# A one-off set-up step in a pipelined attention block: the shift of b1, W1's scaling, and the order of the third step

## The chip, the cores and the metric

The kernel runs on one core of a Trainium2 chip. A core has five engines with instruction streams of their own: TensorE (PE in the profile, its weight loads PEld), VectorE (DVE), ScalarE (ACT), GpSimd (POOL) and SyncE (SP). SP only issues transfers here; ACT computes and issues transfers too. An engine works through its stream in order, so an instruction that waits holds everything behind it, and an issued transfer counts as an instruction in that stream. The metric is the device time of one execution in microseconds (us). The kernel before took 1613.01 us (median of 3 runs, 1612.12 to 1615.33).

## The reference

One cross-attention block over 128 sequences of 128 tokens with 256 features, in float32, 16 heads of 16. The mask is strictly causal (`allowed = j < i`), and the first query row gets zero attention. Cut to what matters:

```python
q = query @ Wq + bq;  k = ctx @ Wk + bk;  v = ctx @ Wv + bv        # by heads
attn = softmax(where(j < i, q k^T / 4, -1e30)); attn[row 0] = 0
x   = layer_norm(query + (attn v) @ Wo + bo, ln1_g, ln1_b)
ffn = relu(x @ W1 + b1) @ W2 + b2                                  # 256 -> 1024 -> 256
out = layer_norm(x + ffn, ln2_g, ln2_b)
```

## The kernel before

**Pairs and steps.** Two sequences make a pair p (64 pairs, `NP`). `step(p)`, line 785, runs for p = 2 to 62 and is a software pipeline over neighbouring pairs: the scores and the softmax of p, the weighting of the values, the output projection and the first layer norm of p-1, the projections of p+1, the hidden layer of p-2 (`hidden`, line 631) and the second feed-forward product of p-3 (`second`, line 652). Lines 674 to 776 are a start-up that does pairs 0 and 1 in another order. Step 2 is the first call, so "the third step" of the change's name is the work of pair 2, and step 3 follows it. In step 2 there is no pair -1, so in the place of `second` it carries leftovers of pairs 0 and 1.

**Softmax.** The scores come in two parts: hi = 1 (queries 64 to 127 against 128 keys, tile `sm1`, two halves of 8 heads) and hi = 0 (queries 0 to 63 against 64 keys, `sm0`). Each part is masked by DVE (line 345), its negated row maximum taken by DVE (356) and added by POOL (357), exponentiated by ACT (364), summed by DVE (376), inverted (377), and multiplied by POOL (378). The profile leaves buffer numbers out and calls both tiles `sm`.

**The turn.** DVE transposes the weights in 32x32 blocks into `tb` (391), and sixteen transfers of 96 KB bring the blocks to their places in `pT` (406): eight issued by SP (line 849), eight by ACT, a few after each group of `hidden` (`share`, line 867). PE then multiplies `pT` with the values in the following step (`weigh`, 438 and 448, tile `pc`), ACT copies the result to `cxT` (460), and PE projects it (`po`, 467). For pair 1 the turn is made on PE instead (`turn_on_pe`, 410). The normalised x1 of a pair is also turned through memory: four transfers to a scratch buffer and one back (`across`, 237 and 240, tiles `x1t` and `x1T`), all on SP.

**Folding the first layer norm.** `hidden` reads x1 without gain and shift. Instead W1 is multiplied once by the gain (`scale_w1`, 583, ACT) and b1 becomes b1e = b1 + ln1_b @ W1: PE computes the product (`fold_norm1`, 559, tile `ps_b1`), ACT copies its four rows to `b1s` (572), eight SP transfers of 512 bytes each turn the rows into columns of `b1e_c` (`add_b1`, 578), and POOL adds b1 (581). Pair 0 is an exception: its copy to `x1T` applies gain and shift (624), so its `hidden` uses the unscaled W1 and b1, and W1 must not be scaled before `hidden(0)` is over. `hidden(1)`, in step 3, is the first that needs b1e and the scaled W1. A second constant, `be1b_r` = ln1_b + b2, is made by POOL (837) and used by `residual1` (511: two POOL operations that make x1 with gain and shift plus b2), for pairs 0 and 1 in step 2.

**What sets the order.** `tc.manual_schedule` keeps the order of the calls on each of the five engines; the framework only adds waits. Every transfer of the two queues raises one of eight completion semaphores, DMAHW0 to DMAHW7, given out in rotation in the order in which the compiled program lists the transfers of both queues (which is not the order of the calls). A transfer is issued only when the previous transfer with the same semaphore has landed, whichever queue that one is on. PSUM has four single banks in rotation (`bank`) and two pairs for scores (`pair`).

Of the kernel before, what the change touches and what calls it, by code (L numbers as in the profile page):

```python
# [10 lines left out]
ALU = mybir.AluOpType  # L11
# [8 lines left out]
def tile_cross_attention_block(  # L20
# [22 lines left out]
    nc = tc.nc  # L43
# [6 lines left out]
    FC = DFF // P  # L50
    TP = 2 * P
    NS = P // 32
    HH = H // 2
    NP = B // 2
# [92 lines left out]
    b1_c = column(b1, "b1_c")  # L147
# [5 lines left out]
    be1_r = row(ln1_b, "be1_r")  # L153
    b2_r = row(b2, "b2_r")
# [94 lines left out]
    def add_bo(p):  # L249
        st = states[p]  # L250
        st["xb"] = proj.tile([P, 2, D], F32, tag="xb", name=f"xb_{p}")
        nc.gpsimd.tensor_tensor(
            st["xb"], tokens_of[p // 2][:, p % 2 * 2 : p % 2 * 2 + 2], bov_r[:, None, :].to_broadcast([P, 2, D]), ALU.add
        )
# [85 lines left out]
    def mask(p, hi, t):  # L340
        st = states[p]
        part = slice(t * HH, (t + 1) * HH)
        n = P if hi else HP
        no = neg.rearrange("p u j -> p (u j)") if hi else neg[:, 1, :]
        nc.vector.tensor_tensor(  # L345
            st["sm", hi][:, part, :].rearrange("p (r n) j -> p r n j", r=2),
            st["sps", hi][t][:, :, : 4 * n].rearrange("p r (n j) -> p r n j", j=n),
            no[:, None, None, :].to_broadcast([P, 2, 4, n]),
            ALU.add,
        )  # L350

    def maximum(p, hi, part):
        st = states[p]
        n = P if hi else HP
        sm, nmx = st["sm", hi], st["nmx", hi]
        nc.vector.tensor_reduce(nmx[:, part], sm[:, part, :], AX.X, ALU.max, negate=True)  # L356
        nc.gpsimd.tensor_tensor(  # L357
            sm[:, part, :], sm[:, part, :],
            nmx[:, part, None].to_broadcast([P, part.stop - part.start, n]), ALU.add,
        )  # L360

    def exponential(p, hi, part):
        sm = states[p]["sm", hi]
        nc.scalar.activation(sm[:, part, :], sm[:, part, :], AF.Exp)  # L364
# [45 lines left out]
    def turn_on_pe(p, hi, ts):  # L410

        st = states[p]
        sm = st["sm", hi].rearrange("p h j -> p (h j)")
        if "pT" not in st:
            pT = soft.tile([P, NS, (H + HH) * 32], F32, tag="pT", name=f"pT_{p}")
            st["pT"] = pT.rearrange("p i (n a) -> p i n a", a=32)
        for t in ts:
            pt = bank(f"ptp{hi}_{p}_{t}")
            for i in range(4):
                at = (4 * t + i) * P  # L420
                nc.tensor.transpose(pt[:, i * P : (i + 1) * P], sm[:, at : at + P], ident)  # L421
            n = 4 * t if hi else H + 4 * t
            nc.scalar.copy(
                st["pT"][:, :, n : n + 4, :].rearrange("p i n a -> p n i a"),
                pt.rearrange("p (n i a) -> p n i a", i=NS, a=32),
            )
# [132 lines left out]
    def fold_norm1():  # L559


        ps = bank("ps_b1")
        n = DFF // NS
        for k in range(KC):
            for j in range(NS):
                nc.tensor.matmul(
                    ps[32 * j : 32 * j + 1, :n], be1_c[:, k : k + 1],
                    w1[:, k, j * n : (j + 1) * n], start=(k == 0), stop=(k == KC - 1),
                )
        for j in range(NS):  # L570
            at = slice(32 * j, 32 * j + 1)
            nc.scalar.copy(b1s[at], ps[at, :n])

    def add_b1():

        for f in range(FC):
            j, u = f // 2, f % 2
            nc.sync.dma_start(
                b1e_c[:, f : f + 1], b1s[32 * j : 32 * j + 1, u * P : (u + 1) * P]
            )  # L580
        nc.gpsimd.tensor_tensor(b1e_c, b1e_c, b1_c, ALU.add)

    def scale_w1():
        for k in range(KC):
# [29 lines left out]
    def turn_x1_on_pe(p):  # L614
        st = states[p]
        x1T = ffn.tile([P, NS, 4 * 32], F32, tag="x1T", name=f"x1T_{p}")
        st["x1T"] = x1T.rearrange("p i (s k a) -> p s i k a", s=2, k=KC)
        pt = transposed(st["x1"], f"ptn_{p}").rearrange(
            "p (k s i a) -> p k s i a", k=KC, s=2, i=NS
        )  # L620
        for k in range(KC):
            if p == 0:

                nc.scalar.activation(
                    st["x1T"][:, :, :, k, :], pt[:, k], AF.Identity,
                    bias=be1_c[:, k : k + 1], scale=g1_c[:, k : k + 1],
                )
            else:
                nc.scalar.copy(st["x1T"][:, :, :, k, :], pt[:, k])  # L629

    def hidden(p, fs, between=None):
        st = states[p]
        if fs[0] == 0:
            st["hT"] = ffn.tile([P, FC, TP], F32, tag="hT", name=f"hT_{p}")
        for f in fs[::2]:
            ph = bank(f"ph_{p}_{f}")
            for i in range(2):
                for k in range(KC):
                    nc.tensor.matmul(  # L639
                        ph[:, i * TP : (i + 1) * TP].rearrange("p (s i a) -> p s i a", s=2, a=32),  # L640
                        w1[:, k, (f + i) * P : (f + i + 1) * P], st["x1T"][:, :, :, k, :],
                        start=(k == 0), stop=(k == KC - 1),
                    )
            for i in range(2):
                nc.scalar.activation(  # L645
                    st["hT"][:, f + i, :], ph[:, i * TP : (i + 1) * TP], AF.Relu,
                    bias=(b1e_c if p else b1_c)[:, f + i : f + i + 1], scale=1.0,
                )
            if between:
                between(f)  # L650
# [100 lines left out]
    mask(1, 1, 1)  # L751
    maximum(1, 1, TWO)
    add_bo(0)
    turn_on_pe(0, 0, range(2))
    for which in "xc":
        tokens(2, which)
# [27 lines left out]

    def step(p):
        nonlocal waiting
        soon = p + 1 < NP
        if p > 2:
            load_ahead(p)
        scores(p, 1)  # L790
        mask(p, 1, 0)
        maximum(p, 1, ONE)
        if p > 2:
            second(p - 3, 0)
        else:
            turn_x1_on_pe(0)
            fold_norm1()
            turn_on_pe(1, 1, range(4))
            hidden(0, range(FC // 2))
            turn_on_pe(1, 0, range(2))  # L800
        mask(p, 1, 1)
        maximum(p, 1, TWO)
        exponential(p, 1, ONE)
        summed = []
        if p > 2:
            second(p - 3, 1)
            if p + 2 < NP:
                tokens(p + 2, "c")
        else:
            for which in "xc":  # L810
                tokens(3, which)
            add_bo(1)
            load_ahead(2)
            load_tokens(2)
        sums(p, 1, ONE)
        exponential(p, 1, TWO)
        if p > 2:
            second_sum(p - 3)
            summed = [p - 3]
        sums(p, 1, TWO)  # L820


        weigh(p - 1)
        context(p - 1)
        scores(p, 0)
        if soon:
            queries(p + 1)
        mask(p, 0, 0)
        mask(p, 0, 1)
        maximum(p, 0, ALL)  # L830
        exponential(p, 0, ALL)
        turn(p, 1, 0)
        turn(p, 1, 1)
        for q in waiting:
            finish(q)
        if p == 2:
            nc.gpsimd.tensor_tensor(be1b_r, be1_r, b2_r, ALU.add)
            residual1(0)
            add_bo(2)
        attention_out(p - 1)  # L840
        attention_sum(p - 1)
        sums(p, 0, ALL)
        attention_stats(p - 1)
        if p + 2 < NP:
            tokens(p + 2, "x")
            if p == 2:
                tokens(p + 2, "c")
        turn(p, 0, 0)
        bring(p, nc.sync, range(NS * NS // 2))
        keys(p + 1)  # L850
        norm1(p - 1)
        turn_x1(p - 1)
        if p == 2:
            add_b1()
        values(p + 1)
        values_out(p + 1)
        for q in waiting:
            store(q)
        add_bo(p + 1)
        residual1(p - 1)  # L860
        for q in summed:
            stats(q, states[q]["t2"], 2)
        for q in summed:
            scale_and_shift(q)
        at = NS * NS // 2

        def share(f):
            nonlocal at
            n = 0 if f == 0 else NS * NS - at if f == FC - 2 else NS // 2
            bring(p, nc.scalar, range(at, at + n))  # L870
            at += n

        hidden(p - 2, range(0 if p > 2 else FC // 2, FC), share)
        if p == 2:
            scale_w1()
        for q in summed:
            norm2(q)
        waiting = summed
# [127 lines left out]
```

## Time and profile before

| what | value |
|---|---|
| median of 3 runs | 1613.01 us |
| the profiled execution, as timed | 1615.05 us |
| its span, first to last instruction | 1613.3 us |
| busy over the span: PE, DVE, POOL, ACT | 98%, 85%, 79%, 47% |
| PE time in the chain that ended last | 94% |
| start of the scores of pairs 2, 3, 4, 5 on PE | 38.70, 62.73, 110.33, 134.66 us |
| mean granted clock of TensorE | 0.992 |

A profile line gives engine, source line, operation, and tiles out<-in. "Idle before, releaser" is the time for which an engine waited and what ended it. The chain that ended last is followed back from the last instruction, so shares in it are shares of time that nothing else hid. Windows are times from the span's start. The profiled execution took 2.04 us more than the median, and 1.75 us of its time lies outside the span.

### The profile page before, as it was taken

How to read it: one execution, taken by the hardware profiler on the slowest of the kernel's cores; microseconds unless marked ns; L12 is line 12 of the kernel's file. 1: busy time of each engine (PE TensorE's matmuls, PEld its weight loads, DVE VectorE, ACT ScalarE, POOL GpSimd, SP SyncE). 2: the span in 40 equal slices, each digit the busy share in tenths (PEclk: the TensorE clock that was granted, in tenths of full speed). 3: DMA queues.
4: the chain of work that ended last, by engine and by line, in shares of the span. 5: the costliest groups of instructions: out<-in, count | busy, mean ns of one | idle time of the engine just before them, and what ended most of it. 6: DMA issues, size and time to landing. Idle time of an engine off the chain costs nothing.

```text
span 1613.3 us, 41269 instructions
## 1 busy us (share of the span) xinstructions
PE 1579.5 (98%) x16512; PEld 1330.4 (82%) x16512; DVE 1370.9 (85%) x1988; ACT 755.9 (47%) x1498; POOL 1282.6 (79%) x1106
## 2 busy tenths in 40 slices
PE   8869999999999999999999999999999999999998
PEld 6658888888888888888888888888888888888887
DVE  7668988988889889889889889888888889889862
ACT  5434444444444445445455455445445445445442
POOL 6568888878888888888888888788788888888882
PEclk9979999999999999999999999999999999999999
DMA  9345565565655655655655655655655655654430
GB/s 196 81 92 134 127 145 132 129 149 129 140 131 131 143 145 132 141 137 126 143 145 128 145 132 126 147 139 124 142 133 128 155 144 120 152 129 110 116 83 27
DMA packets 480512, 210.12 MB, mean 130 GB/s; under 512 B 349249, under 2 KB 448833, under 8 KB 480321
## 3 DMA queue, kind: packets, MB, share of 16 engines
q1 hardware_dynamic: 371952, 134.55, 37.3%
q10 hardware_dynamic: 108368, 72.92, 17.4%
q8 instruction: 131, 2.15, 0.6%
q14 instruction: 61, 0.49, 0.1%
HBM read 70.00 MB, written 33.03 MB: 64 GB/s over the span
## 4 chain that ended last, share of the span: by engine, by line
PE 94%; POOL 2%; DVE 2%; DMA 1%; SPq 1%; ACT 1%; issue 0%; POOLq 0%; ACTq 0%; DVEq 0%
PE ph L639 27%; PE py L657 26%; PE pq L260 7%; PE po L467 7%; PE pv L292 7%; PE pk L260 7%; PE pss L326 6%; PE pc L448 3%; PE pc L438 2%; POOL sm L357 1%; DVE sm L345 0%; POOL sm L378 0%; DVE nmx L356 0%; PE ptp L421 0%; DMA x1t<-tbx 0%
## 5 line engine op out<-in xcount | busy, mean ns | idle before, releaser
L357 POOL TENSOR_TENSOR sm<-sm,nmx 128x1024 f32<-128x1024 f32 x192 | 364.2, 1897 | 122.6 <-DVE nmx L356 122.2
L657 PE MATMUL py<-w,hT 128*128 128x256 f32 x2016 | 453.2, 382 | 1.8 <-ACT hT L645 1.7
L639 PE MATMUL ph<-x1T,w 128*128 128x256 f32 x2048 | 453.0, 379 | 0.8 <-ACT x1T L629 0.8
L657 PEld LDWEIGHTS py<-w,hT 128*128 128x128 f32 x2016 | 377.6, 190 | 75.1 <-issue 19.0
L378 POOL TENSOR_TENSOR sm<-sm,rs 128x1024 f32<-128x1024 f32 x192 | 364.3, 1899 | 89.8 <-DVE rs L377 88.3
L639 PEld LDWEIGHTS ph<-x1T,w 128*128 128x128 f32 x2048 | 389.0, 190 | 54.0 <-ACT x1T L629 1.0
L376 DVE TENSOR_REDUCE su<-sm 128x8 f32<-128x1024 f32 (+1 forms) x192 | 233.6, 1217 | 86.7 <-ACT sm L364 84.3
L645 ACT ACTIVATE hT<-ph,b1e_c 128x256 f32<-128x256 f32 x504 | 208.4, 471 | 210.3 <-PE ph L639 107.3
L364 ACT ACTIVATE sm<-sm 128x1024 f32<-128x1024 f32 x192 | 200.9, 1053 | 216.2 <-POOL sm L357 215.6
L345 DVE TENSOR_TENSOR sm<-pss,neg 128x1024 f32<-128x1024 f32 (+1 forms) x256 | 235.2, 939 | 53.3 <-PE pss L326 51.7
L391 DVE STREAM_TRANSPOSE tb<-sm 128x1024 f32<-128x1024 f32 x183 | 220.0, 1227 | 29.5 <-POOL sm L378 29.5
L356 DVE TENSOR_REDUCE nmx<-sm 128x8 f32<-128x1024 f32 (+1 forms) x192 | 234.3, 1220 | 6.6
L536 ACT ACTIVATE t<-t,nb,sd 128x256 f32<-128x256 f32 x124 | 67.7, 593 | 187.9 <-DMA pT<-tb 121.6
L467 PE MATMUL po<-wo,cxT 128*128 128x256 f32 x512 | 123.0, 384 | 16.2 <-ACT cxT L460 16.1
L260 PE MATMUL pq<-xT,wq 128*128 128x256 f32 x512 | 128.0, 393 | 0.0
L467 PEld LDWEIGHTS po<-wo,cxT 128*128 128x128 f32 x512 | 98.1, 192 | 30.4 <-ACT cxT L460 17.0
L282 ACT ACTIVATE kT<-pk,bkh,half 128x256 f32<-128x256 f32 x252 | 120.6, 558 | 0.9 <-PE pk L260 0.9
L292 PE MATMUL pv<-wv,cT 128*128 128x256 f32 x512 | 120.9, 379 | 0.0
L260 PE MATMUL pk<-cT,wk 128*128 128x256 f32 x504 | 119.7, 380 | 0.0
L326 PE MATMUL pss<-kT,qT 32*64 32x256 f32 (+1 forms) x4096 | 117.0, 335 | 0.4 <-ACT kT L706 0.2
L271 ACT ACTIVATE qT<-pq,bqs_c 128x256 f32<-128x256 f32 x128 | 53.6, 470 | 122.8 <-PE pq L260 122.8
L260 PEld LDWEIGHTS pq<-xT,wq 128*128 128x128 f32 x512 | 92.7, 191 | 21.0 <-issue 10.8
(92 smaller groups left out, 1752.1 us busy)
## 6 DMA issues: line engine op xcount, KB each, us to landing
pT<-tb ACTq DMA_DIRECT2D x488, 96.0 KB, 2.7
pT<-tb SPq DMA_DIRECT2D x488, 96.0 KB, 2.9
out_dram<-t ACTq DMA_DIRECT2D x63, 256.0 KB, 2.5
xb<-in_x_dram SPq DMA_DIRECT2D x124, 128.0 KB, 4.5
cb<-in_ctx_dram SPq DMA_DIRECT2D x124, 128.0 KB, 4.5
x<-in_x_dram SPq DMA_DIRECT2D x31, 512.0 KB, 5.5
x1t<-tbx SPq DMA_DIRECT2D x248, 64.0 KB, 2.2
x1T<-x1t SPq DMA_DIRECT2D x62, 256.0 KB, 3.2
```

Of the source, the lines that this page charges most:

```text
L260: nc.tensor.matmul(ps[:, m * TP : (m + 1) * TP], w[:, k, m * P : (m + 1) * P], src[:, k, :], start=(k == 0), stop=(k == KC - 1),)
L292: nc.tensor.matmul(pv[:, s * D : (s + 1) * D], st["cT"][:, k, s * P : (s + 1) * P], wv[:, k, :], start=(k == 0), stop=(k == KC - 1),)
L326: nc.tensor.matmul(sps[r // 2][s * HP : (s + 1) * HP, r % 2, m * 2 * n : (m + 1) * 2 * n].rearrange("p (e j) -> p e j", e=2), st["qT"][str ...
L345: nc.vector.tensor_tensor(st["sm", hi][:, part, :].rearrange("p (r n) j -> p r n j", r=2), st["sps", hi][t][:, :, : 4 * n].rearrange("p r ...
L356: nc.vector.tensor_reduce(nmx[:, part], sm[:, part, :], AX.X, ALU.max, negate=True)
L357: nc.gpsimd.tensor_tensor(sm[:, part, :], sm[:, part, :], nmx[:, part, None].to_broadcast([P, part.stop - part.start, n]), ALU.add,)
L376: nc.vector.tensor_reduce(su, sm[:, part, :], AX.X, ALU.add)
L378: nc.gpsimd.tensor_tensor(sm[:, part, :], sm[:, part, :], rs[:, :, None].to_broadcast([P, part.stop - part.start, n]), ALU.mult,)
L391: nc.vector.transpose(st["tb"][:, :, at : at + 256].rearrange("p j (n a) -> p n j a", a=32), st["sm", hi].rearrange("p h j -> p (h j)")[:, ...
L467: nc.tensor.matmul(po[:, s * D : (s + 1) * D], cxT[:, k, s, :], wo[:, k, :], start=(k == 0), stop=(k == KC - 1),)
L639: nc.tensor.matmul(ph[:, i * TP : (i + 1) * TP].rearrange("p (s i a) -> p s i a", s=2, a=32), w1[:, k, (f + i) * P : (f + i + 1) * P], st[ ...
L657: nc.tensor.matmul(st["py"][:, s * D : (s + 1) * D], st["hT"][:, f, s * P : (s + 1) * P], w2[:, f, :], start=(f == 0), stop=(f == FC - 1),)
```

## The change

The product for b1 goes from the start of step 2 to behind its second set of scores, and the eight transfers follow it directly, which puts them on SP ahead of the eight `pT` transfers and of the turn of x1. POOL's addition of b1 and W1's scaling on ACT go to step 3, behind its second scores. POOL's `be1b_r` goes to the start-up, and `residual1(0)` behind `add_bo(3)`. In step 2 the first half of `hidden(0)` comes before the turn of pair 1 on PE, ACT's first exponential comes between the copies of that turn, and ACT issues its eight `pT` transfers together at the end of `hidden(0)`. The steps from 4 on keep their order.

```diff
@@ add_b1
             nc.sync.dma_start(
                 b1e_c[:, f : f + 1], b1s[32 * j : 32 * j + 1, u * P : (u + 1) * P]
             )
-        nc.gpsimd.tensor_tensor(b1e_c, b1e_c, b1_c, ALU.add)
@@ start-up
     add_bo(0)
+    nc.gpsimd.tensor_tensor(be1b_r, be1_r, b2_r, ALU.add)
     turn_on_pe(0, 0, range(2))
@@ step
         if p > 2:
             second(p - 3, 0)
-        else:
-            turn_x1_on_pe(0)
-            fold_norm1()
-            turn_on_pe(1, 1, range(4))
-            hidden(0, range(FC // 2))
-            turn_on_pe(1, 0, range(2))
-        mask(p, 1, 1)
-        maximum(p, 1, TWO)
-        exponential(p, 1, ONE)
-        summed = []
-        if p > 2:
+            mask(p, 1, 1)
+            maximum(p, 1, TWO)
+            exponential(p, 1, ONE)
             second(p - 3, 1)
             if p + 2 < NP:
                 tokens(p + 2, "c")
         else:
+            turn_x1_on_pe(0)
+            hidden(0, range(FC // 2))
+            turn_on_pe(1, 1, range(2))
+            mask(p, 1, 1)
+            maximum(p, 1, TWO)
+            exponential(p, 1, ONE)
+            turn_on_pe(1, 1, range(2, 4))
+            turn_on_pe(1, 0, range(2))
             for which in "xc":
                 tokens(3, which)
...
         scores(p, 0)
-        if soon:
-            queries(p + 1)
+        if p == 2:
+            fold_norm1()
+            add_b1()
+        if p == 3:
+            scale_w1()
+            nc.gpsimd.tensor_tensor(b1e_c, b1e_c, b1_c, ALU.add)
+        queries(p + 1)
...
         if p == 2:
-            nc.gpsimd.tensor_tensor(be1b_r, be1_r, b2_r, ALU.add)
-            residual1(0)
             add_bo(2)
...
         turn_x1(p - 1)
-        if p == 2:
-            add_b1()
         values(p + 1)
...
         add_bo(p + 1)
+        if p == 2:
+            residual1(0)
         residual1(p - 1)
...
-            n = 0 if f == 0 else NS * NS - at if f == FC - 2 else NS // 2
+            n = NS * NS - at if f == FC - 2 else 0 if f == 0 or p == 2 else NS // 2
             bring(p, nc.scalar, range(at, at + n))
...
-        if p == 2:
-            scale_w1()
```

More of the change, by code (lines that the diff above doesn't have):

```diff
@@ L786, in step @@
         nonlocal waiting
-        soon = p + 1 < NP
         if p > 2:
@@ L814, in step @@
             load_tokens(2)
+        summed = []
         sums(p, 1, ONE)
```

## The prediction

> **What bounds the kernel now.** I read the page first: PE is busy 98% of the span, so only time in which PE idles or runs slowly can be won. The slices show where that is.
>
> ```profile
> PE   8869999999999999999999999999999999999998
> ...
> PEclk9979999999999999999999999999999999999999
> ```
>
> The hole is slice 3 (81 to 121 us), where the clock falls too. Then PE's waits from 40 to 110 us, with POOL's and SP's (waiting line <- releasing line: us, times, longest):
>
> ```profile
> PE po L467 <- ACT cxT L460: 14.7, 1, 14.7
> PE pc L438 <- DMA pT<-tb: 2.5, 1, 2.5
> PE py L657 <- ACT hT L645: 1.7, 1, 1.7
> ...
> POOL b1e_c L581 <- DMA b1e_c<-b1s: 20.3, 1, 20.3
> ...
> SPq L406 <- DMA pT<-tb: 2.1, 2, 1.8
> ```
>
> PE waits 14.7 us for `cxT`, but ACT is not the cause. The timeline (start, us) shows it:
>
> ```profile
> 66.67 7.10 SPq L406 DMA_DIRECT2D pT<-tb  x8
> ...
> 73.86 2.01 SPq L237 DMA_DIRECT2D x1t<-tbx  x4
> ...
> 79.16 0.38 SPq L240 DMA_DIRECT2D x1T<-x1t  x1
> ...
> 79.59 5.07 SPq L578 DMA_DIRECT2D b1e_c<-b1s  x8
> ...
> 86.50 0.20 POOL L581 TENSOR_TENSOR b1e_c<-b1e_c,b_c 128x8 f32<-128x8 f32 x1 [20.27 <-DMA b1e_c<-b1s]
> ...
> 92.36 1.06 ACT L364 ACTIVATE sm<-sm 128x1024 f32<-128x1024 f32 x1 [17.99 <-POOL sm L357]
> ...
> 95.79 3.78 PE L467 MATMUL po<-wo,cxT 128*128 128x256 f32 x8 [14.69 <-ACT cxT L460]
> ```
>
> The eight b1 transfers stand on SP behind `pT` and the turn of x1. POOL, in order, stands at its addition until 86.50; behind it are `xb`, `x1b` and the maxima of pair 3, behind these ACT's exponentials, and behind these in ACT's stream the copy to `cxT`, though `pc` was done by 77.4.
>
> The scores of pair 3 start at 62.73, those of pair 4 at 110.33, those of pair 5 at 134.66. A normal step takes 24.3, so step 3 has 23.3 us too much. From 110 to 1580 us PE's waits add up to 1.6 us, so what is won before 110.33 stays won. The clock is in two windows of the same work, `pc` to `pq`, here and a step later (us; busy by engine; PEclk):
>
> ```profile
> 75.42:81.11 5.69, 5.66 (x136) 4.44 (x136) 0.00 (x0) 0.00 (x0) 0.00 (x0) 0.70 0.26 70
> ...
> 118.48:122.57 4.09, 4.09 (x138) 3.62 (x138) 3.99 (x8) 1.56 (x2) 3.38 (x2) 1.00 0.90 162
> ```
>
> After 2.46 us without work PE needs 1.60 us more for the same.
>
> **The change, part by part.** I work out when pair 4's scores start.
>
> *POOL's addition, one step later.* The 20.3 us wait goes: at its new place (about 79) the last b1 transfer must have landed, which it has (73, below). `xb` (1.27) and two `x1b` (2.55 each, one of them moved here) run from 63.8 to 70.2; before, `xb` and one `x1b` ran from 86.7 to 90.5. The maxima of pair 3 end at 74.0 (before 94.2), the exponentials at 75.1, `cxT` follows when `pc` is done. The 14.7 us wait disappears, unless `pc` itself is late. The addition (0.20) lies before the maximum of `sm0`, which waits for DVE until 83: covered.
>
> *`be1b_r` to the start-up.* 0.73 us on POOL, between `xb` (ends 31.9) and the maximum waiting for DVE until 34.40. It needs b2's row, issued at 19.72; the transfer behind it on the same semaphore starts at 32.38, so it has landed by then and the addition ends by 33.2: nothing. With no cover it would be 0.7.
>
> *Step 2, PE.* The first `hidden(0)` products wait only for `x1T` (first half 41.95, second 42.45): 42.0 to 45.8. The turn of pair 1 follows, 45.8 to 49.0. ACT runs `hT` to 46.7, two copies to 47.7, the exponential to 48.8, four copies to 50.9, the second exponential to 51.9. `pc` waits for the last copy: 50.95 against 50.09 before, ending 52.45; scores to 53.1; the product for b1 (1.04) now here: `pq` starts 54.1 instead of 52.17. So PE is 1.9 late: `po` 55.9, `pk` 57.6, `pv` 59.4, `hidden` 61.1, pair 3's scores 64.65 (before 62.73), `py` 65.7. But `py` had waited 1.75 for `hT`, since ACT had two `pT` issues, waiting for `tb`, between the groups; now `hT` ends at 65.5 and `py` runs through, 65.7 to 72.8, as before (72.96). Cost by then: nothing. PE's new wait at 40.4 (1.6 us) would cost 1.6 more if the clock fell after it; after the 1.75 at 66.6 it stayed at 1.00.
>
> *Step 2, the softmax.* The exponential at 48.8 (before 50.9) brings the maximum of `sm0` to 56.15 (before 56.97), and three operations (3.27 us) leave POOL before the last multiplication. It waits for DVE's sum, which waits for the exponential at 59.15: 60.95 to 62.85 (before 63.33 to 65.2). `tb` is ready at 64.45, before 66.52. ACT's four `b1s` copies (1.47) fall between `cxT` and `qT`, at 54.1 to 55.6, where ACT was free.
>
> *SP: the b1 transfers ahead of `pT`.* This decides. The compiled program lists ACT's `pT` transfers ahead of SP's b1 transfers, and they share semaphores (number that each waits for):
>
> ```
> ACT pT  2nd waits HW1=96    raises HW1 to 112
> SP  b1  6th waits HW1=112   raises HW1 to 128
> ACT pT  3rd raises HW3 to 112;   SP b1 7th waits HW3=112
> ACT pT  8th waits HW1=128
> SP  pT  3rd waits HW2=128 (ACT pT 5th);  SP pT 8th waits HW7=128 (ACT pT 7th)
> ```
>
> The trace of before shows such a hold: an ACT `pT` issue starts at 67.91, lands at 70.69, and SP's next issue is at 70.71.
>
> ```profile
> 67.91 2.78 DMA pT<-tb
> ...
> 70.71 0.51 SPq L406
> ```
>
> Five b1 transfers go out from 54.5 to about 58, unheld (0.60 each). The sixth stands until ACT's second `pT` lands, and ACT issues all eight only after `hT` (65.55): second at 66.2, landing 2.8 later at 69.0. SP then issues three b1 (0.64 each) to 70.9; they land 2.0 after issue, by 72.4. Then eight `pT`, of which some wait for ACT's: the third for the landing at 71.8, the eighth for 74.0. At 0.6 each that ends with an issue at 75.3, landing 2.2 later (73.17 to 75.38 before): 77.5. ACT's last is issued at 71.8 and lands by 75. So `pc` starts at 77.5, against 75.42. Ends: landings of 2.0 everywhere give 76.7; 3.0 and one more lap of waiting, 79.
>
> *After that.* PE stands 4.7 us (72.8 to 77.5). I take the measured 5.69 for `pc` to `pq`, the nearest row: 83.2. Ends: full clock 4.09 (81.6); half clock throughout, as after the long wait, where 95.79 to 101.8 took 6.0 for 3.5 of work, about 6.6 (84.1). ACT has `cxT` at 80.2, W1's scaling (2.19) to 82.4, `qT` to 84.2; the exponential of `sm0` comes at 85.3, and `hidden` needs W1 only at 88.5, so the scaling costs nothing; uncovered it would be 2.2. The turn of x1 follows `pT`: 76 to 78, back by 85, before 88.5. From `pq`'s end to the next scores a normal step takes 12.09 (122.57 to 134.66): 95.3. Against 110.33: -15.0.
>
> The profiled execution, 1615.05, is 2.04 above the median; the same difference from the median 1613.0 gives **1598.0 us**.
>
> [...]
>
> **Rivals.** *The transfers hide.* If SP were not held by ACT's issues, SP's `pT` would start at 64.5 and land at 73.8 (7.1 of issues, 2.2): `pc` at 73.8, `pq` at full clock to 77.9, scores of pair 4 at 90.0: -20.3, 1592.7. For it: the b1 product is ready at 54. Against: the semaphores, and ACT's stream has `hT` ahead of every `pT`.
>
> *Part of it is lost again.* ACT waits for SP and SP for ACT; a lap more (2.8 landing, 0.6 issue) and half clock (1.0) leave about -10.6, 1602.4. For it: in steps 2 and 3 both queues are held. Against: each hold named above ends with one landing.
>
> *Slower.* The compiled listing deals the semaphores out differently in steps 4 to 11 too; from step 12 on it is that of before. If in these eight steps `pT` landed after `py`'s end, each would cost. In step 4 ACT's last `pT` issue starts at about 114.8; with 2.8 it lands at 117.6, and `pc` starts at 118.48, so there is 0.9 us of slack. It decides against the change from 1.9 us a step (15.0 / 8) upward: 2.5 a step is 20.0, and 1598.0 + 20.0 = 1618. Against: PE waited 1.6 us in 1470 us, while the semaphores stood in every rotation.
>
> **How the numbers follow.** The sum as worked out: 0.77; transfers hidden: 0.08; partly lost: 0.11; slower: 0.04, of which 0.01 ends within 0.2% (3.2 us, about what a measurement of this kernel can tell from no change). The likeliest's own range is 1596 to 1600.5 (its ends: `pc` at 76.7 or 79, clock -1.6 or +1.0, runs within 1). The range takes in both near rivals and leaves out the last: 1592.5 to 1602.5. Faster 0.96, same 0.01, slower 0.03.
>
> **What would show it.** Right: the b1 transfers split in two groups, five before 60 and three after 68; no POOL wait at b1's addition; `po` after `pq` without a wait; one PE wait of 4 to 5 us for `pT` near 73; pair 4's scores near 95. Wrong: SP's b1 issues in one run (first rival); pair 4's scores after 98; PE waits for `pT` beyond 110.

## The result, and the profile after

The changed kernel takes 1601.42 us (median of 4 runs, 1598.13 to 1602.61) beside 1614.17 us of the kernel before in the same comparison: ratio 0.9919, 95% interval 0.9899 to 0.9939, so it is 12.75 us faster. In a second comparison (the first experiment below) it took 1599.72 us beside 1614.92: ratio 0.9907, interval 0.9895 to 0.9919, 15.2 us faster. The forecast was 1598.0, with 1592.5 to 1602.5 as range. The profiled execution is the quickest of the first four, 1598.13 us with a span of 1596.4; its counterpart before had 1615.05 and 1613.3.

The page's slices of the changed kernel: the hole in slice 3 (80 to 120 us) is gone, and in these slices the granted clock of TensorE no longer falls below 0.9.

```profile
PE   8899999999999999999999999999999999999998
...
PEclk9999999999999999999999999999999999999999
```

The waits of PE, POOL and SP from 40 to 100 us (waiting line <- releasing line: us, times, longest us):

```profile
PE pc L438 <- DMA x1t<-tbx: 3.9, 1, 3.9
PE pc L438 <- ACT pT L423: 1.9, 2, 1.7
PE ph L638 <- ACT x1T L623: 1.6, 1, 1.6
...
POOL sm L378 <- DVE rs L377: 7.8, 6, 2.8
POOL sm L357 <- DVE nmx L356: 6.3, 3, 4.2
...
SPq L578 <- DMA vd<-vz: 8.9, 1, 8.9
...
SPq L578 <- ACT b1s L572: 3.0, 1, 3.0
SPq L578 <- DMA pT<-tb: 1.6, 2, 1.2
```

POOL no longer waits at the addition of b1, where it stood 20.3 us, and PE no longer waits 14.7 us for `cxT`. PE's longest wait is now 3.9 us at `pc`. Its releaser is given as a transfer of x1's turn, but that is only the transfer behind the last `pT` on SP: `pc` reads `pT`, and the last `pT` was issued at 74.3, with 2.2 us as the median to landing. On SP the new long wait is at b1 (line 578), for the landing of `vd`.

The timeline from 53 to 95 us (start, us, engine, line, operation, count, and in brackets idle time before and releaser), with SP's b1 issues asked for in three stretches so that its groups come apart:

```profile
54.40 1.21 SPq L578 DMA_DIRECT2D b1e_c<-b1s  x2
...
61.86 0.60 ACTq L306 DMA_DIRECT2D vd<-vz  x1
...
64.58 1.80 SPq L578 DMA_DIRECT2D b1e_c<-b1s  x3
...
65.25 5.32 ACTq L406 DMA_DIRECT2D pT<-tb  x7
65.48 7.17 PE L656 MATMUL py<-w,hT 128*128 128x256 f32 x32
...
67.61 2.02 SPq L578 DMA_DIRECT2D b1e_c<-b1s  x3
...
69.73 5.12 SPq L406 DMA_DIRECT2D pT<-tb  x8
...
76.55 0.43 PE L438 MATMUL pc<-pT,vd 128*32 128x64 f32 x16 [3.89 <-DMA x1t<-tbx]
...
78.28 0.20 POOL L831 TENSOR_TENSOR b1e_c<-b1e_c,b_c 128x8 f32<-128x8 f32 x1
...
79.38 2.19 ACT L584 ACTIVATE w<-w,g_c 128x1024 f32<-128x1024 f32 x2
...
82.02 1.89 PE L467 MATMUL po<-wo,cxT 128*128 128x256 f32 x8
...
94.20 1.12 PE L326 MATMUL pss<-kT,qT 32*64 32x256 f32 x32
```

The addition (78.28) and `po` (82.02) run without a wait, W1's scaling lies under PE's work, and pair 4's scores start at 94.20 instead of 110.33. The windows of `pc` to `pq`, and of the rest up to those scores (us, busy by engine, clock, DMA share, GB/s):

```profile
76.52:82.18 5.66, 5.63 (x137) 4.89 (x138) 2.13 (x3) 2.67 (x3) 1.97 (x2) 0.70 0.29 78
82.18:94.20 12.02, 12.02 (x58) 10.29 (x56) 10.61 (x19) 7.13 (x16) 8.07 (x7) 1.00 0.69 151
```

The first shows the clock behind the wait (0.70 in the mean; 5.66 us for work that takes 4.09 at full clock; where in it the clock is half is shown in the last section), the second a normal rest of a step.

What the two steps cost is best read as S4 - S2, from the start of pair 2's scores to that of pair 4's. Before, it was 110.33 - 38.70 = 71.6 us; two normal steps of 24.3 are 48.6, so 23.0 were too much. After, it is 94.20 - 38.95 = 55.3, which leaves 6.7. From pair 4's scores to the end of the span it took 1503.0 before (1613.3 - 110.33) and 1502.2 after (1596.4 - 94.20), so nothing was given back later.

### The profile page after: what moved, and what is told of

It is laid out like the page before. It is cut to its first block, busy times and chain, and to the rows that moved or that the text cites. A ratio compares the mean times of both kernels' runs of the same rounds, so it can differ in the third digit from the quotient of the medians.

```text
span 1596.4 us, 41271 instructions
## 1 busy us (share of the span) xinstructions
PE 1574.0 (99%) x16512; PEld 1327.7 (83%) x16512; DVE 1372.2 (86%) x1988; ACT 755.9 (47%) x1498; POOL 1282.6 (80%) x1106
## 4 chain that ended last, share of the span: by engine, by line
PE 95%; POOL 1%; DVE 1%; ACT 1%; DMA 1%; issue 0%; SPq 0%; POOLq 0%; ACTq 0%; DVEq 0%
PE ph L638 27%; PE py L656 27%; PE pq L260 8%; PE po L467 7%; PE pk L260 7%; PE pv L292 7%; PE pss L326 6%; PE pc L448 4%; PE pc L438 2%; POOL sm L357 0%; POOL sm L378 0%; ACT pT L423 0%; DMA pT<-tb 0%; DVE nmx L356 0%; DVE sm L345 0%
## 5 line engine op out<-in xcount | busy, mean ns | idle before, releaser
L656 PEld LDWEIGHTS py<-w,hT 128*128 128x128 f32 x2016 | 377.6, 190 | 72.8 <-issue 16.7
L515 POOL TENSOR_TENSOR x1b<-x,g_r 128x512 f32<-128x512 f32 x64 | 81.7, 1277 | 34.9 <-DVE x L507 34.9
```

The costliest lines, as they stand in the source:

```text
L656: nc.tensor.matmul(st["py"][:, s * D : (s + 1) * D], st["hT"][:, f, s * P : (s + 1) * P], w2[:, f, :], start=(f == 0), stop=(f == FC - 1),)
```

## The experiments

All are edits of the changed kernel, but for the third. S2, S3 and S4 are the starts of the scores of pairs 2, 3 and 4 on PE in the profiled execution.

**The changed kernel again.** No edit.

> The changed kernel once more, with more executions. Its profiled execution so far had the scores of pair 4 on PE at 94.2 us, 16.1 earlier than before, and it was the quickest of four (1598.1; the others 1600.6 to 1602.6). If what varies lies in steps 2 and 3, another profile has pair 4's scores 2 to 4 us later, and the median stays at 1600 to 1602. If it lies elsewhere, pair 4's scores stand at 94 to 95 again, and the rest of the span is longer than 1502 us.

Measured: 1599.72 us (1597.39 to 1600.04, 5 runs). Its profiled execution had S2 at 40.17 and S4 at 95.67: 55.5, as in the first profile (55.3), and 1502.5 from S4 to the end of its span (1598.2). The two profiles differ by 1.8 us in span, of which 1.2 are there before step 2 begins. So the gain in steps 2 and 3 repeats (16.1 and 16.3 us less than 71.6), and most of what varies is the start-up. In this profile SP's first `pT` issue is at 71.34 and `pc` starts at 78.32 after 4.4 us; `pc` to the end of `pq` took 5.36 at a clock of 0.74.

**b1's product and transfers earlier**, behind the turn of x1 on PE at the start of step 2.

```diff
             turn_x1_on_pe(0)
+            fold_norm1()
+            add_b1()
...
         scores(p, 0)
-        if p == 2:
-            fold_norm1()
-            add_b1()
```

> The change, but with b1's product and its eight transfers at the start of step 2, ahead of hidden(0). In the compiled program no b1 transfer then shares a semaphore with an earlier ACT pT transfer. If the hold by ACT's pT transfers sets when pT is complete: SP's b1 issues stand in one run near 44 to 49, pc of pair 2 starts at 74 to 75 instead of 76.5, pair 4's scores at 90.5 to 92.5 instead of 94.2, and the time is 2 to 3.5 us below the changed kernel. If pT is late for another reason (ACT's own eight, or the landing itself): pc stays at 76 to 77, and the time is that of the changed kernel within 1 us.

Measured: 1600.64 us, ratio 0.9912 (0.9899 to 0.9925); S4 - S2 = 93.98 - 39.01 = 55.0. The b1 transfers went out in one run, at 43, and yet nothing was won. SP's timeline of this kernel:

```profile
43.02 5.10 SPq L578 DMA_DIRECT2D b1e_c<-b1s  x8
...
64.14 0.39 SPq L100 DMA_DIRECT2D x<-in_x_dram  x1
68.97 5.67 SPq L406 DMA_DIRECT2D pT<-tb  x8
```

and the waits of SP and PE:

```profile
SPq L100 <- DMA vd<-vz: 12.8, 1, 12.8
...
SPq L406 <- DMA pT<-tb: 5.3, 3, 4.3
...
PE pc L438 <- DMA x1t<-tbx: 4.6, 1, 4.6
```

The holds came back with other transfers: the load of x, now in the place of a b1 transfer in the rotation, stands until `vd` has landed, and SP's first `pT` waits 4.3 us for one of ACT's. `pc` waits 4.6 us as before. So it is not b1's place on SP that makes `pT` late, but that ACT issues its transfers late and SP shares the semaphores with them.

**The kernel before with POOL's addition alone moved**; the transfers stay behind `pT` and the turn of x1.

```diff
@@ add_b1 (kernel before)
-        nc.gpsimd.tensor_tensor(b1e_c, b1e_c, b1_c, ALU.add)
@@ step
         scores(p, 0)
+        if p == 3:
+            nc.gpsimd.tensor_tensor(b1e_c, b1e_c, b1_c, ALU.add)
         queries(p + 1)
```

> The kernel before with one edit: POOL's addition to b1e goes to step 3, behind its second scores; product, transfers, W1's scaling and the order of step 2 stay. If the gain is POOL no longer standing in step 2: POOL's wait of 20 us shrinks to 5 to 8, po has no wait of 14.7, pair 4's scores start at 95 to 97, and the time is 1 to 3 us above the changed kernel, so 10 to 12 below before. If the place of the transfers on SP matters most: b1e still lands at 86, the maximum of pair 3's second scores waits for it behind the addition, pT of pair 3 is complete only near 103, and the time is 5 us or more above the changed kernel.

Measured: 1602.11 us, ratio 0.9927 (0.9914 to 0.9940); S4 - S2 = 94.72 - 38.62 = 56.1. Its waits of POOL and PE:

```profile
POOL b1e_c L826 <- DMA cb<-in_ctx_dram: 5.3, 1, 5.3
...
PE pc L438 <- DMA x1t<-tbx: 2.5, 1, 2.5
PE py L656 <- ACT hT L644: 1.8, 1, 1.8
PE ph L638 <- ACT kT L282: 1.4, 1, 1.4
```

Of the 16.3 us that the whole change wins here, 15.5 come from this one moved instruction, though the transfers are almost as late as ever (issued from 77.7, before from 79.6) and POOL still waits 5.3 us at the addition; the profile names a transfer of the context, issued behind the b1 transfers, as the one that ended this wait. The wait costs far less at the later place, because the first two maxima of pair 3 are through before it, but it is not free: the maximum of `sm0` starts behind the addition at 86.20, ACT's exponential waits 6.2 us for it, the copies to `kT` follow that, and PE waits 1.4 us for them at `ph` (the last line). From the end of `pq` to pair 4's scores it takes 13.7 us here and 12.0 in the changed kernel. In medians the moved instruction is worth 12.8 us of 15.2; the two intervals overlap.

**PE kept busy through its wait**: 28 transposes of the identity behind `second` in step 3, into a bank that nothing reads.

```diff
             second(p - 3, 1)
+            if p == 3:
+                warm = bank("warm_3")
+                for i in range(28):
+                    nc.tensor.transpose(warm[:, i % 4 * P : (i % 4 + 1) * P], ident, ident)
```

> The changed kernel with 28 transposes of the identity on PE behind the second product of step 3 (extra work whose result nobody reads), so that PE does not stand while pT lands. If pc to pq took 5.7 instead of 4.1 because PE had stood before: the clock stays at 1.00 there, pair 4's scores come 1.3 to 1.7 us earlier (92.5 to 93), the time falls by as much. If the slowness has another cause, or the filler itself delays pc: pair 4's scores at 94 or later, the time the same or above.

Measured: 1597.86 us (1596.61 to 1604.03), ratio 0.9904 (0.9889 to 0.9920); S4 - S2 = 93.71 - 38.63 = 55.1. PE's timeline of this kernel:

```profile
72.19 3.22 PE L801 MATMUL warm<-ident 128*128 128x128 f32 x28
76.78 0.43 PE L438 MATMUL pc<-pT,vd 128*32 128x64 f32 x16 [1.37 <-DMA x1t<-tbx]
77.00 0.66 PE L448 MATMUL pc<-pT,vz 128*32 128x64 f32 x32
...
80.35 1.35 PE L260 MATMUL pq<-xT,wq 128*128 128x256 f32 x5 [0.55 <-issue]
```

and its window of `pc` to `pq`:

```profile
76.75:81.70 4.95, 4.37 (x137) 3.58 (x138) 2.64 (x4) 2.67 (x3) 1.49 (x3) 1.00 0.22 53
```

The clock stays at 1.00, with the same `pc` start relative to S2 (38.2; 37.6 and 38.2 in the two profiles of the changed kernel). So the slow stretch behind the wait is the clock (0.70 and 0.74 from `pc` to `pq` in the two profiles of the changed kernel), and here PE standing idle is what brings it on. The gain is smaller than forecast: the stretch takes 4.95 us instead of 5.66 and 5.36, and not 4.09. The rest lies in `pq`, which takes 2.82 us instead of 1.99, round a gap of 0.55 for which the profile shows no releaser, and S4 - S2 falls by only 0.2 to 0.4. In time it can't be told from the changed kernel.

**Useful work in the wait**: in step 3, the second scores and the queries ahead of `weigh`.

```diff
+        if p == 3:
+            scores(p, 0)
+            queries(p + 1)
         weigh(p - 1)
         context(p - 1)
-        scores(p, 0)
+        if p != 3:
+            scores(p, 0)
...
-        queries(p + 1)
+        else:
+            queries(p + 1)
```

> The changed kernel, with PE's order altered in step 3 alone: the second scores of pair 3 (0.7 us) and the queries of pair 4 (1.7 us) come ahead of the weighting of pair 2, where PE stands for pT. If what is left to win there is PE standing, and the half clock after it: pc of pair 2 starts with a wait of 1 to 2 instead of 3.9 to 4.4, the clock stays at 1.00, and pair 4's scores start 51.5 to 52.5 us after pair 2's (55.3 and 55.5 in the two profiles of the changed kernel), so the time is 3 to 4 us below it. If something else ends step 3 (POOL's softmax of pair 3, x1T, W1's scaling): pair 4's scores stay at 54.5 or more after pair 2's, the time within 1 us.

Measured: 1597.05 us (1595.26 to 1598.28), ratio 0.9889 (0.9875 to 0.9904); S4 - S2 = 93.53 - 40.77 = 52.8. PE's timeline:

```profile
74.43 0.69 PE L326 MATMUL pss<-kT,qT 32*64 32x128 f32 x32
75.05 1.99 PE L260 MATMUL pq<-xT,wq 128*128 128x256 f32 x8
79.01 0.43 PE L438 MATMUL pc<-pT,vd 128*32 128x64 f32 x16 [1.96 <-DMA x1t<-tbx]
79.23 0.66 PE L448 MATMUL pc<-pT,vz 128*32 128x64 f32 x32
...
81.25 1.99 PE L467 MATMUL po<-wo,cxT 128*128 128x256 f32 x8 [0.69 <-ACT cxT L460]
```

The scores and `pq` (2.6 us) lie inside the wait, which shrinks to 2.0, and here `po` waits 0.7 us for `cxT`, which it no longer has `pq` to hide. That is 2.5 us less than the changed kernel in S4 - S2, a little short of the forecast. In time it can't be told from the changed kernel: its interval, 0.9875 to 0.9904, overlaps 0.9895 to 0.9919.

**All sixteen `pT` of step 2 on SP**, so that ACT issues none.

```diff
-        bring(p, nc.sync, range(NS * NS // 2))
+        bring(p, nc.sync, range(16 if p == 2 else NS * NS // 2))
...
-        at = NS * NS // 2
+        at = 16 if p == 2 else NS * NS // 2
```

> The changed kernel, with all sixteen pT transfers of step 2 on SP and none on ACT. If ACT's pT transfers are what held SP's b1 and pT: SP's eight b1 issues run in one piece, 54.4 to about 59.5, SP's first pT issue follows tb at 64 instead of 69.7, the sixteen take 10.2, and pc starts at 75.5 to 76.5, so the time stays within 1.5 us of the changed kernel though the hold is gone. If SP was held by something else: the b1 issues stay split, the first pT issue stays near 70, pc comes at 81 or later, and the time is 4 us or more above.

Measured: 1603.47 us, ratio 0.9927 (0.9910 to 0.9943); S4 - S2 = 97.94 - 38.35 = 59.6. I had expected b1's issues in one run. SP's timeline says otherwise:

```profile
55.36 11.97 SPq L578 DMA_DIRECT2D b1e_c<-b1s  x8
67.43 10.14 SPq L406 DMA_DIRECT2D pT<-tb  x16
```

and so do the waits of SP, with the one of PE that follows:

```profile
SPq L578 <- DMA vd<-vz: 6.8, 1, 6.8
...
SPq L406 <- DMA pT<-tb: 2.0, 1, 2.0
...
PE pc L438 <- DMA pT<-tb: 5.3, 2, 4.8
```

SP still stands 6.8 us, for `vd`, which is ACT's transfer too, and then the sixteen issues (10.14 us) are one behind another, so that the last block lands near 79. Even issued from 64.3, where `tb` is ready here, the sixteen would end at 74.4 and the last block would land at about 76.1 (an estimate from these rows, with 2.2 us to landing), which is hardly earlier than `pc` starts in the changed kernel (76.5). So one queue alone brings `pT` little. Part of the loss is something else: PE ran step 2 at a lower clock here (0.79 from 48 to 56 us, 1.00 in the changed kernel, with the same waits ahead of it), and S3 - S2 was 27.0 instead of 25.5.

**POOL's addition back in step 2**, just ahead of the values, with everything else as in the changed kernel.

```diff
         if p == 3:
             scale_w1()
-            nc.gpsimd.tensor_tensor(b1e_c, b1e_c, b1_c, ALU.add)
...
         turn_x1(p - 1)
+        if p == 2:
+            nc.gpsimd.tensor_tensor(b1e_c, b1e_c, b1_c, ALU.add)
         values(p + 1)
```

> The changed kernel, with POOL's addition to b1e back at its old place in step 2, ahead of xb and x1b. If the gain comes from POOL not standing behind the turn of x1, early transfers alone bring most of it: POOL waits 7 to 8 us at the addition, until about 71, po of pair 2 waits 0.5 to 2, pair 4's scores start 56 to 57 us after pair 2's (71.6 in the kernel before), and the time is 0.5 to 2 us above the changed kernel. If the later place of the addition is what counts: POOL's wait stays near 20 us and the time is within 5 us of the kernel before.

Measured: 1603.78 us, ratio 0.9932 (0.9916 to 0.9949); S4 - S2 = 98.94 - 41.03 = 57.9. Its waits:

```profile
POOL b1e_c L856 <- DMA pT<-tb: 9.2, 1, 9.2
...
PE pc L438 <- DMA x1t<-tbx: 4.2, 1, 4.2
PE po L467 <- ACT cxT L460: 2.3, 1, 2.3
```

This is the change without POOL's later addition: the rest of it, above all the earlier transfers, brings 13.7 us (71.6 - 57.9) even with the addition at its old step. POOL's wait falls from 20.3 to 9.2 us, and of that only 2.3 reach PE; both are a little more than forecast, and so is S4 - S2. The two parts overlap: 15.5 and 13.7 us singly, 16.3 together. The smaller pieces of the rest (the order of step 2, W1's scaling, `be1b_r`, `residual1(0)`) were not run by themselves.

**A version from what was found**: b1 early (second experiment), the order of step 3 with useful work in the wait (fifth), and 12 of the 16 `pT` of step 2 on SP, 4 on ACT.

```diff
-        bring(p, nc.sync, range(NS * NS // 2))
+        bring(p, nc.sync, range(12 if p == 2 else NS * NS // 2))
...
-        at = NS * NS // 2
+        at = 12 if p == 2 else NS * NS // 2
```

> Three edits on the changed kernel: b1's product and transfers at the start of step 2, twelve pT transfers of step 2 on SP and four on ACT, and the PE order of step 3 with the second scores and the queries ahead of the weighting. If SP held by ACT and PE standing are what is left: x2's load goes out near 51, SP's pT start at 64 and are complete by 74 to 74.5, PE has nearly no wait at pc, pair 4's scores start 49.5 to 50.5 us after pair 2's, and the time is 4.5 to 6 us below the changed kernel. If x1T or POOL's chain ends step 3 instead: 52 or more after pair 2's, and no better than the kernel with the altered PE order alone.

Measured: 1593.47 us (1592.98 to 1597.21), ratio 0.9873 (0.9858 to 0.9888): 21.2 us below the kernel before (1614.63 in this comparison); the interval lies below that of the changed kernel, 0.9895 to 0.9919. S4 - S2 = 89.39 - 39.41 = 50.0, 1.4 above two normal steps. PE's timeline:

```profile
64.99 7.17 PE L656 MATMUL py<-w,hT 128*128 128x256 f32 x32
72.09 0.69 PE L326 MATMUL pss<-kT,qT 32*64 32x128 f32 x32
72.71 1.99 PE L260 MATMUL pq<-xT,wq 128*128 128x256 f32 x8
74.64 0.66 PE L438 MATMUL pc<-pT,vd 128*32 128x64 f32 x16
...
77.10 1.99 PE L467 MATMUL po<-wo,cxT 128*128 128x256 f32 x8 [0.69 <-ACT cxT L460]
```

SP's first `pT` goes out at 64.57 here and `pc` starts without a wait. The split into twelve and four was not run by itself, so its share of the gain is not shown. What is left of PE's waits is the 0.7 us at `po`, and the waits of step 2 (0.7 at `ph`, 1.9 at `pc`).

## Why the prediction was right

The steps beside what the two profiles of the changed kernel show, in us:

| step | forecast | first profile | second profile |
|---|---|---|---|
| S3 - S2 | 64.65 - 38.70 = 26.0 | 25.5 | 25.5 |
| end of `py` | 72.8 | 72.65 | 73.88 |
| SP's sixth b1 issue | 69.0 | 67.6 | 68.9 |
| SP's first `pT` issue | 70.9 | 69.73 | 71.34 |
| start of `pc`, after S2 | 77.5 - 38.7 = 38.8 | 37.6 | 38.2 |
| PE's wait at `pc` | 4.7 | 3.9 | 4.4 |
| `pc` to end of `pq` | 5.69 | 5.66 | 5.36 |
| from there to S4 | 12.09 | 12.02 | 12.02 |
| S4 - S2 | 95.3 - 38.7 = 56.6 | 55.3 | 55.5 |

*POOL's addition.* Right: no wait, and the exponentials, `cxT` and `po` follow. The third and seventh experiments show that either part of the change takes PE's 14.7 us at `po` away almost alone: nothing of it is left there in the third (which has 1.4 us at `ph` instead), and 2.3 us in the seventh.

*SP's split.* The hold by ACT's `pT` was right, the first part was wrong. "Five b1 transfers go out, unheld" fails: two went out, and the third stood 8.9 us until `vd` had landed (issued by ACT at 61.86; SP goes on at 64.58). The compiled listing has it, as I read it now: `vd`'s transfer waits for an earlier value of DMAHW5, and the third b1 transfer waits for DMAHW5 next. I had listed the holds between b1 and `pT` only. It cost nothing, because the sixth b1 transfer waits for ACT's second `pT` anyway, and that hold came out as forecast, 1.4 us earlier. ACT's second `pT` was issued at 65.25, not 66.2, and the hold ended 2.36 us later (67.61), not 2.8. This earlier end fits the 0.6 to 1.2 us by which `pc` came ahead of its forecast.

*The clock.* Taking 5.69 from the row of before came out well: 5.66 and 5.36. That was in part luck, since what the wait cost depended on how much of the half-clock stretch lay behind the start of `pc` (last section). In all seven profiles with a wait of 2.5 to 4.8 us at `pc`, `pc` to the end of `pq` took 5.36 to 6.67 us, against 4.09 at full clock. After 1.4 us in the fourth experiment the clock stayed at 1.00, and after 2.0 in the fifth the parts of `pc` took 0.43 and 0.66 us, as in the fourth.

*W1's scaling, `be1b_r`.* Both hidden, as forecast: the scaling (79.38 to 81.57) ends before `pq` does, and `be1b_r` (32.96) is followed by 0.95 us in which POOL waits for DVE.

*The sum.* Forecast -15.0. In the traces steps 2 and 3 are 16.3 and 16.1 us shorter, 1.1 to 1.3 more than forecast: in the first profile nearly all of it from the terms ahead of `pc`, in the second 0.6 from these and 0.3 from the stretch behind the wait. In medians it is 12.75 and 15.2. The forecast of 1598.0 took 15.0 off the median of 1613.01 that was known then. In the comparison that median is 1614.17, and the gain is 2.25 less; together these are the 3.4 us by which the first median, 1601.42, lies above the forecast, inside the stated range but outside that of its likeliest case, 1596 to 1600.5. The second, 1599.72, lies in both. Why the first gain is the lower its profile can't say, since that is the quickest of the four executions; the others had spans up to 1600.9. In the ten profiles S2 ranges from 38.4 to 41.0, and S4 to the end from 1501.2 to 1503.7, nearly as widely, so they do not single out a stage. The granted clocks on record are 0.996, 0.997 and 0.998 for the three slower executions and 0.998 for the profiled one: a lower clock may be behind two of the three, but not behind the last. The cause stays open.

*The rivals.* "The transfers hide" fails on the split in the timeline. It is nearly what the last experiment makes on purpose: `pc` at 74.6 without a wait, S4 at 89.4, beside 73.8 and 90.0 in that rival. "Part of it is lost again" would have had S4 past 98. "Slower", through steps 4 to 11, is excluded by the 1502.2 us behind S4 and by PE's waits there, 2.6 us in all up to 1580.

What stays open: the 0.55 us gap at `pq` with PE kept busy, why the clock fell in step 2 with sixteen `pT` on SP, what makes the start-up vary, and why the first comparison showed the smaller gain.

## What to carry to other kernels

An in-order engine that waits for a late transfer, as POOL did here for 20.3 us, costs what stands behind it in the stream; moving the one waiting instruction behind work that others need, here POOL's addition of 0.2 us, won 15.5 of the 16.3 us. When two queues draw completion semaphores from one rotation, list for every held transfer which transfer of the other queue had that semaphore before: here moving or removing transfers shifted the hold to a neighbour rather than ending it (12.8 us at the load of x in the second experiment, 6.8 at b1 in the sixth), so look at when the other engine issues. A PE wait that stays can be filled with later work that is already ready: in the fifth experiment 2.6 us of such work cut the wait at `pc` to 2.0 us, left the parts of `pc` at 0.43 and 0.66 us, which they took at a clock of 1.00 in the fourth, and shortened S4 - S2 by 2.5 us.

## What I had not expected of the hardware

The same waits did not give the same clock. In step 2 all kernels with the new order have PE waits of 0.7 or 1.6 us at `ph` and 1.7 at the following `pc`; the window from 48 to 56 us shows 1.00 in the changed kernel and 0.79 in the one with sixteen `pT` on SP, which had the same two waits, 1.6 and 1.7, and in which PE was busy for as long, 6.14 us (as above: us, busy by engine, clock, DMA share, GB/s; the changed kernel first). Why the clock differs is not shown.

```profile
48.00:56.00 8.00, 6.14 (x160) 4.59 (x159) 6.09 (x9) 5.85 (x12) 6.45 (x5) 1.00 0.67 134
...
48.00:56.00 8.00, 6.14 (x150) 4.28 (x150) 5.18 (x7) 4.70 (x10) 5.76 (x4) 0.79 0.65 134
```

Nor did the clock fall where a wait began or ended. In step 3 of the changed kernel it is full through PE's wait and for the first 0.60 us of `pc`, then half for 3.41 us, then full again (four windows, from the end of `py` to the end of `pq`). In the second profile of that kernel it is 0.95 already in the 6.30 us that end with the wait, and 0.74 from `pc` to `pq` (the last two windows).

```profile
72.65:76.52 3.87, 0.01 (x1) 0.00 (x1) 3.32 (x5) 1.27 (x2) 2.96 (x3) 1.00 0.63 153
76.52:77.12 0.60, 0.57 (x41) 0.60 (x45) 0.00 (x0) 0.00 (x0) 0.60 (x1) 1.00 0.57 143
77.12:80.53 3.41, 3.41 (x105) 2.82 (x94) 0.51 (x1) 1.62 (x3) 1.37 (x2) 0.50 0.15 36
80.53:82.18 1.65, 1.65 (x9) 1.47 (x8) 1.62 (x3) 1.04 (x2) 0.00 (x0) 1.00 0.48 142
...
72.00:78.30 6.30, 1.88 (x9) 1.34 (x8) 4.79 (x7) 2.11 (x2) 5.40 (x4) 0.95 0.63 157
...
78.29:83.65 5.36, 5.33 (x137) 4.81 (x138) 1.79 (x3) 2.49 (x3) 1.41 (x2) 0.74 0.22 54
```

In the kernel before, the clock is 0.50 from 76.49 to 79.91, 1.00 from there to 83.32, 2.2 us into PE's wait of 14.7, and 0.50 again to 100.39, of which PE works 4.6 us.

This also gives the price of the wait at `pc`, 5.66, 5.36 and 5.36 us for `pc` to the end of `pq` after 3.9, 4.4 and 4.2 us of waiting (the two profiles of the changed kernel, and the one with POOL's addition back), against 4.09 at full clock. About half of the time for which PE works at half clock is lost: that is 3.41 us in the first profile, and about 2.8 in the second if its clock was full or half there too (a mean of 0.74 over 5.36 us), so 1.7 and 1.4 us as an estimate, beside 1.57 and 1.27 measured. In the second profile part of the half-clock stretch was over before `pc` began (0.95 in the window ahead of it), so the longer wait cost less.

The start-up varies by up to 2.7 us between executions (S2 from 38.35 to 41.03), which is more than several of these edits are worth. In the profile with 41.03 POOL's `xb` started at 33.46, in that of before at 30.65, so the difference is there before `be1b_r`, the one instruction that the change adds to the start-up; what makes it was not traced.
